# First batch's softmax and rows transposed on TensorE, its product in column blocks, its statistics as x lands

## The chip, the cores and the metric

The kernel runs on one core of a Trainium2 chip. The metric is the device time of one execution in microseconds, the median of three runs. The profile is one further execution, taken by the hardware profiler. Its times are microseconds from the start of the span. The engines are called PE (TensorE), DVE (VectorE), ACT (ScalarE), POOL (GpSimd) and SP (SyncE, which here only issues DMAs).

## The reference

The model is one block: a cross-attention whose keys come from a context, then an attention and mixture-of-experts block. There are four batches of 512 rows and 512 features. Cut to what matters:

```python
def xattn(logits, features, Wq, bq, Wk, bk):        # logits (4,512,512), features (4,512,256)
    query = features @ Wq.T + bq                    # 128 features
    key = features @ Wk.T + bk
    attention = softmax(query @ key.T, axis=-1)     # (512, 512)
    return einsum('bln,bmn->blm', logits, attention)

def ffn(hidden, ...):
    h = rmsnorm(hidden, ln1_w)
    q, k, v = h @ wq, h @ wk, h @ wv                # 16 heads of 128
    ao = causal_softmax(q @ k.T / sqrt(128)) @ v @ wo
    x = hidden + ao
    t = rmsnorm(x, ln2_w)
    # 16 experts, the best 6 of each row, and a shared expert
    return x + routed(t) + shared(t)

x = x + xattn(layernorm(x), ctx)
x = x + ffn(layernorm(x), ...)
```

## The kernel before, in words

Each number is held as a pair of 16-bit halves, a high half and a remainder. `split` makes the pair: ACT writes the high half, DVE the remainder. A product of two pairs takes three matmuls (`mm3`). Biases and scales ride along.

**Cross-attention, `xattn(b)`.** This is a Python generator, one for each batch; `step(b, n)` runs it for n yields. Its work for a batch is, in order: split the context (`ctp`); project queries and keys (tiles `xq`, `xqk`); bring in x turned, in two halves (`turned`), and make its pair `lnp` (`turn`: the high half on ACT, the remainder on POOL); four energies (`en`), each with a maximum on DVE, an exponential on ACT, a reciprocal and a split into `pn`; `pn` turned into `ptp`, here by a DMA transpose that SP issues (`flip`). `stats` takes mean and variance of the rows of x with DVE (`bn_stats`, four tiles), lets POOL take the power -1/2, and makes `nb`. `center` adds `nb` to x on POOL. Then four products `xm` of `lnp` with `ptp`, each followed by an update of x, a second layer norm (`mv`, `r`, `hu`, `hd`), and the normalised rows as a pair `hh`, which is turned into `hT` by `flip`. Products share the two PSUM banks with the tag w; banks a and s have three each.

**Heads.** The attention loop runs over 64 heads of four batches, first those of batches 0 and 1. `queries`, `values`, `scores`, `attend` and `project` are its stages. `fetch` brings in the weights of a head the first time: a load into a staging tile, `split`, and a write of the pair to a scratch tensor in HBM (`wqk_d`, `wv_d`, `wo_d`), from which later batches read. The staging pool `stg` has two tiles with the tag st. The context of a batch, both halves of its turned x (batch 0's turned x apart) and the weights take turns in them, so a load waits until the last reader of the tile before is through.

**What sets the order.** The kernel is written as one program, and a scheduler puts the instructions into one fixed queue for each engine. `after(ins, first)` adds an order between two instructions. SP's queue carries loads and transposes, POOL's queue carries POOL's own arithmetic and the scratch writes. `warm` issues matmuls with no use of their result. Batch 0 runs through the generator at once (`step(0, 99)`), then the small loads (`ln2b`, `zrow`, `g32`, `gtp`) and the first nine yields of batch 1 are issued, and batch 1's last twelve yields follow two for each of the first six heads. The loop of head 0 splits `values` and `queries` in halves, so that the first half needs only half of `hT`.

Of the kernel before, what the change touches and what calls it, by code (L numbers as in the profile page):

```python
# [9 lines left out]
F16 = mybir.dt.float16  # L10
F32 = mybir.dt.float32
# [44 lines left out]
def xattn_moe_block_kernel(ctx: ExitStack, tc: tile.TileContext, x, xT, ctxT, wqkx, bqk, ln1, ln2,  # L56
# [32 lines left out]

    def flip(o, i):  # L90
        return nc.sync.dma_start_transpose(out=o, in_=i)

    def after(ins, first):
        tc.add_manual_dep(ins.ins, first.ins.name,
# [90 lines left out]
    def warm(n, first=None):  # L185
        ps = bank("w", "warm")
        for _ in range(n):
            ins = nc.tensor.matmul(ps, onesm, zero, start=True, stop=True)
            if first:
                after(ins, first)  # L190

    warm(10)
    ct0 = ctx_load(0)
    wx32 = at_.tile([P, 2 * CC * P], F32, tag="f", name="wx32")
# [8 lines left out]
    def xattn(b):  # L203
# [4 lines left out]
            nc.sync.dma_start(t, xT[b, j])  # L208
            return t

        if b == 0:
            xT32 = [turned(j) for j in range(2)]
        xt = (ap_ if b else x2p).tile([P, NT, D], F32, tag="xt" if b else "x2", name=f"xt{b}")
        nc.sync.dma_start(xt, x[b].rearrange("(t p) d -> p t d", p=P))
        if b == 0:
            nc.sync.dma_start(ln1b, ln1.partition_broadcast(P))
            for nm, src in (("wqk0", wqk[0]), ("wv0", wv[0])):
                t = vp.tile([P, NT, 2, GW], F16, tag="vt", name=f"{nm}_st")
                early_st[nm] = t.rearrange("p t a d -> p (t a d)").bitcast(F32)
                nc.sync.dma_start(early_st[nm], src)  # L220
        ctp = ap_.tile([P, 2, CC, S], F16, tag="lnp", name="ctp")
        for j, ins in enumerate(split(ctp[:, 0], ctp[:, 1], ct32, HS)):
            if b == 1:
                after(ins, zz["calm"][j])
        spare = dict(pm=[(he, "pe3"), (xp, "h2"), (he, "pe3"), (xp, "x1t")],
                     pn=[(hq, "qk0"), (hq, "qk1"), (he, "pn3"), (rp, "h2p")], hh=[(he, "pn3"), (rp, "h2p")])
        spare.update(hu=spare["pm"], qf=spare["pm"])
# [21 lines left out]
        def stats():  # L249
            mv = asm.tile([P, NT, 2], F32, name="mvs", bufs=2)  # L250
            for m in range(NT):
                st = asm.tile([P, 6], F32, name="st")
                ins = nc.vector.bn_stats(st, xt[:, m, :])
                if b < 2:
                    after(ins, zz["hh", 0] if b else zz["sm", 0][1])
                nc.vector.bn_aggr(mv[:, m, :], st)
            ins = nc.vector.tensor_scalar(rs, mv[:, :, 1], 1e-5, PS * PS, ALU.add, ALU.mult)
            if b == 0:
                zz["calm"] = zz["sm", 0][0], ins
            nc.gpsimd.tensor_tensor(rs, rs, mhalf, ALU.pow)  # L260
            ins = nc.vector.scalar_tensor_tensor(nb, mv[:, :, 0], -PS, rs, ALU.mult, ALU.mult)
            if b == 0:
                zz["nb"] = ins

        def center(t):
            nc.gpsimd.tensor_scalar(xt[:, t, :], xt[:, t, :], nb[:, t:t + 1], None, ALU.add)
# [21 lines left out]
        if b == 0:  # L288
            warm(8, zz["xq"])
            for j in range(2):  # L290
                turn(j, xT32[j])
        else:
            lnp = wide("lnp")
        yield
        for m in range(NT):
            ml = slice(m * P, (m + 1) * P)
            if b:
                if m < 2:
                    turn(m, turned(m))
                elif m == 2:  # L300
                    stats()
                else:
                    for t in range(NT):
                        center(t)
                yield
            ps = bank("s", f"en{b}_{m}")
            last = mm3(ps, [(qk[0][:, 0, ml], qk[0][:, 1, ml], qk[1][:, 0], qk[1][:, 1])])
            nm = asm.tile([P, 1], F32, name="nm")
            ins = nc.vector.tensor_reduce(nm, ps, AX.X, ALU.max, negate=True)
            if b == 1:  # L310
                after(ins, zz["hh", 0])
            pm = tmp("pm", F32)
            sm = asm.tile([P, 1], F32, name="sm")
            nc.scalar.activation(pm, ps, AF.Exp, bias=nm, accum_out=sm)
            rc = asm.tile([P, 1], F32, name="rc")
            nc.vector.reciprocal(rc, sm)
            nc.vector.tensor_scalar(rc, rc, PS, None, ALU.mult)
            pn, hi, lo = pair(tmp("pn", F16))
            zz["sm", b] = split(hi, lo, pm, rc)
            zz["ptp", b] = flip(ptp[:, :, ml], pn)  # L320
            yield
        if b == 0:
            stats()
            after(nc.vector.tensor_scalar(ln1b, ln1b, HS, None, ALU.mult), zz["calm"][1])
            for t in range(NT):
                center(t)
            warm(22, last)
        if b < 2:
            x2s[b] = x2p.tile([P, NT, D], F32, tag="x2", name="x2")
        hT[b] = hpool.tile([P, 2 * C, S], F16, tag="hT", name=f"hT{b}")  # L330
        for t in range(NT):
            ps = bank("w", f"xm{b}_{t}")
            tl = slice(t * P, (t + 1) * P)
            xv = xt[:, t, :]
            zz["xm", b, t] = mm3(ps, [(lnp[:, c, tl], lnp[:, C + c, tl], ptp[:, c], ptp[:, C + c]) for c in range(C)])
            nc.vector.scalar_tensor_tensor(xv, ps, rs[:, t:t + 1], xv, ALU.mult, ALU.add)
            q = nc.gpsimd if b else nc.sync
            q.dma_start(x1_d[b][:, t, :], xv)
            st = asm.tile([P, 6], F32, name="st")
            nc.vector.bn_stats(st, xv)  # L340
            mv = asm.tile([P, 2], F32, name="mv")
            nc.vector.bn_aggr(mv, st)
            r2 = asm.tile([P, 2], F32, name="r2")
            nc.vector.tensor_scalar(r2[:, 0:1], mv[:, 1:2], 1e-5, None, ALU.add)
            nc.vector.tensor_scalar(r2[:, 1:2], mv[:, 1:2], 1.0 + 1e-6, 1e-11, ALU.mult, ALU.add)
            nc.gpsimd.tensor_tensor(r2, r2, mhalf[:, :2], ALU.pow)
            hu = tmp("hu", F32)
            nc.vector.scalar_tensor_tensor(hu, xv, mv[:, 0:1], ln1b, ALU.subtract, ALU.mult)
            yield
            nb = asm.tile([P, 1], F32, name="nb")  # L350
            nc.vector.scalar_tensor_tensor(nb, mv[:, 0:1], -1.0, r2[:, 0:1], ALU.mult, ALU.mult)
            hd = x2s[b][:, t] if b < 2 else tmp("hd", F32)
            nc.gpsimd.tensor_scalar(hd, xv, r2[:, 0:1], nb, ALU.mult, ALU.add)
            if b >= 2:
                q.dma_start(hid_d[b][:, t, :], hd)
            if stop == "A":
                nc.sync.dma_start(out[b, tl], hd)
            yield
            hh, hi, lo = pair(tmp("hh", F16))
            zz["hh", b] = split(hi, lo, hu, r2[:, 1:2])[1]  # L360
            zz["hT", b] = flip(hT[b][:, :, tl], hh)
            yield

    if stop == "A":
# [7 lines left out]
        for _ in range(n):  # L372
            next(bg[b], None)

    step(0, 99)
    ln2b = const.tile([P, D], F32, name="ln2b")
    nc.sync.dma_start(ln2b, ln2.partition_broadcast(P))
    after(nc.vector.tensor_scalar(ln2b, ln2b, HS, None, ALU.mult), zz["calm"][1])
    zrow = xp.tile([1, D], F32, tag="x1t", name="zrow", bufs=1)
    nc.vector.memset(zrow, 0.0)  # L380
    nc.gpsimd.dma_start(y_d[0:1, :], zrow)
    nc.gpsimd.dma_start(yo_d[0:1, :], zrow)
    g32 = const.tile([P, C * E], F32, name="g32")
    nc.sync.dma_start(g32, gate)
    gtp = const.tile([P, 2, C, E], F16, name="gtp")
    gtf = gtp.rearrange("p a c e -> p a (c e)")
    for j, ins in enumerate(split(gtf[:, 0], gtf[:, 1], g32, WS)):
        after(ins, zz["calm"][j])
    step(1, 1 + 2 * NT)

    shx = {}

# [13 lines left out]
    def fetch(b, g, pool, tag, n, src, scr, nm):  # L406
# [10 lines left out]
        if first:  # L417
            st_ = early_st[nm]
        else:
            st_ = stg.tile([P, 1024], F32, tag="st", name=f"{nm}_st")  # L420
            ins = nc.sync.dma_start(st_[:, :n], src)
            if nm == "wqk1":
                after(ins, zz["hT", 0])
        for j, ins in enumerate(split(w[:, 0], w[:, 1], st_[:, :n], WS)):
            if first:
                after(ins, zz["nb"] if j else zz["calm"][0])
        ins = (nc.sync if nm == "wqk0" else nc.gpsimd).dma_start(scr, w.rearrange("p a n -> p (a n)"))
        if nm != "wqk0":
            zz["pad"] = ins
        if nm == "wqk0":  # L430
            after(ins, zz["ptp", 0])
        return w

    pieces = []
# [300 lines left out]
    for n in range(NH + LAG + 1):  # L735
        if n < NH:
            b, h = heads[n]
            if b not in opened:
                opened.add(b)
                step(b, 99)  # L740
                if b == B - 1:
                    shared_pool()
            parts = [queries(b, h)]
            if h % HG == 0:
                parts.append(values(b, h // HG))
            if n == 0:
                parts.reverse()
                for p in parts:
                    next(p)
            for p in parts:  # L750
                for _ in p:
                    pass
# [28 lines left out]
        if H // 2 <= n < H // 2 + E:  # L781
            pad_rows(n - H // 2)
        if n < 6:
            step(1, 2)
        else:
            for _, j in zip(range(2 - n % 2), bring):
                step(j)
# [441 lines left out]
```

## Time and profile before

| what | value |
|---|---|
| median of three runs | 1832.03 us (1832.01 to 1837.33) |
| profiled execution | 1838.93 us |
| its span, first to last instruction | 1837.2 us |
| mean granted clock of TensorE | 0.974 |
| TensorE busy | 1739.6 us, 95% |
| VectorE busy | 1113.9 us, 61% |
| ScalarE busy | 829.5 us, 45% |
| GpSimd busy | 444.8 us, 24% |

The page cuts the span into 40 slices of 46 us and gives each engine's busy share of a slice in tenths. A row of the timeline has the start, the length, the engine, the line of the kernel, the operation, what it writes and reads, and in brackets the idle time of the engine before it with what ended it. A row of the waits has the waiting instruction, what it waited for, the total, the number and the longest. Where a helper such as `split` or `mm3` records the instruction, the line is that of the helper, and the tile tells whose it is.

### The profile page before, as it was taken

The page shows a single profiled execution, that of the slowest core. Times are in us where ns is not written, and L with a number is a line of the kernel's source. Part 1 is how long each engine was busy: PE and PEld are TensorE (multiplying, and loading weights), DVE is VectorE, ACT ScalarE, POOL GpSimd, SP SyncE. Part 2 cuts the span into 40 slices and gives each one's busy share as a digit, 9 for nine tenths or more (in the row PEclk, how much of TensorE's full clock was granted, in tenths as well). Part 3 has the DMA queues.
Part 4 walks back from the last instruction along what each step waited for, and adds up shares of the span by engine and source line. Part 5 has one row for each costly group of instructions (what it writes and reads, how often), then busy time and mean ns, then how long its engine had stood idle before and what let it go on. Part 6 is the DMA issues. An engine that isn't in the chain of part 4 may idle for free. (4 is left out here: it accounts for less than half of the span.)

```text
span 1837.2 us, 27581 instructions
## 1 busy us (share of the span) xinstructions
PE 1739.6 (95%) x9919; PEld 937.2 (51%) x9919; DVE 1113.9 (61%) x2766; ACT 829.5 (45%) x1711; POOL 444.8 (24%) x522
## 2 busy tenths in 40 slices
PE   7899999999986998999999979899999999999998
PEld 3455555555543554645655534345555555555453
DVE  6887777777673774756667625554444434446755
ACT  4555645465432543535445423234444444544431
POOL 5423011130345235000003334400000000025564
PEclk9899999999997998999999989899999999999999
DMA  7977768674675677654437534566454655579766
GB/s 235 228 165 215 160 144 191 159 185 93 136 161 159 151 168 212 134 101 91 86 68 150 130 107 102 199 178 177 138 155 144 178 147 147 148 223 252 217 206 209
DMA packets 392723, 296.23 MB, mean 161 GB/s; under 512 B 334880, under 2 KB 335136, under 8 KB 391808
## 3 DMA queue, kind: packets, MB, share of 16 engines
q1 hardware_dynamic: 359456, 180.32, 42.0%
q0 software_dynamic: 33120, 114.06, 19.6%
q8 instruction: 80, 1.31, 0.3%
q14 instruction: 67, 0.55, 0.1%
HBM read 124.81 MB, written 88.94 MB: 116 GB/s over the span
## 5 line engine op out<-in xcount | busy, mean ns | idle before, releaser
L1105 POOL DMA_INDIRECT yg<-y_d,yrc x96 | 110.5, 1151 | 535.8 <-DVE hf L1008 455.6
L630 ACT ACTIVATE pe<-pe,bnm 128x128 f32<-128x128 f32 (+3 forms) x256 | 142.4, 557 | 161.1 <-DVE bnm L628 156.4
L83 PE MATMUL qk<-hT,wqk 128*128 128x512 f16 (+1 forms) x520 | 197.8, 380 | 5.0 <-DMA hT<-hh 3.8
L86 PE MATMUL qk<-hT,wqk 128*128 128x512 f16 (+1 forms) x520 | 197.9, 381 | 1.1 <-issue 1.1
L87 PE MATMUL qk<-hT,wqk 128*128 128x512 f16 (+1 forms) x520 | 197.8, 380 | 1.1 <-issue 1.1
L74 DVE SCALAR_TENSOR_TENSOR pn<-pe,brc,pn 128x128 f16<-128x128 f32 (+3 forms) x256 | 146.7, 582 | 21.9 <-ACT pn L73 18.6
L628 DVE CUSTOM_DVE_ANT_0 pe<-sc,causal 128x128 f32<-128x128 f32 (+3 forms) x256 | 117.4, 486 | 64.0 <-PE sc L625 57.2
L86 PE MATMUL v<-wv,hT 128*128 128x256 f16 x512 | 141.6, 276 | 6.5 <-issue 6.5
L83 PE MATMUL v<-wv,hT 128*128 128x256 f16 x512 | 141.5, 276 | 6.4 <-issue 5.5
L73 ACT ACTIVATE pn<-pe,brc 128x128 f16<-128x128 f32 (+3 forms) x256 | 133.5, 553 | 30.1 <-ACT pe L630 16.3
L87 PE MATMUL v<-wv,hT 128*128 128x256 f16 x512 | 141.5, 276 | 4.9 <-issue 4.7
L83 PE MATMUL g<-xT,wt 128*128 128x384 f16 (+2 forms) x384 | 127.3, 331 | 0.0
L86 PE MATMUL g<-xT,wt 128*128 128x384 f16 (+2 forms) x384 | 127.3, 331 | 0.0
L87 PE MATMUL g<-xT,wt 128*128 128x384 f16 (+2 forms) x384 | 127.2, 331 | 0.0
L994 ACT ACTIVATE hT_e<-hf 128x384 f16<-128x384 f32 (+3 forms) x96 | 51.1, 532 | 143.9 <-DVE hf L1008 136.2
L73 ACT ACTIVATE qkt<-qk 128x512 f16<-128x512 f32 x128 | 75.0, 588 | 90.5 <-PE qk L87 85.0
L83 PE MATMUL y<-dt,hT_e 128*128 128x512 f16 (+1 forms) x288 | 109.4, 380 | 0.0
L87 PE MATMUL y<-dt,hT_e 128*128 128x512 f16 (+1 forms) x288 | 108.9, 378 | 0.0
L86 PE MATMUL y<-dt,hT_e 128*128 128x512 f16 (+1 forms) x288 | 108.9, 378 | 0.0
L662 DVE SCALAR_TENSOR_TENSOR x<-wo,x 128x512 f32<-128x512 f32 x128 | 87.5, 687 | 32.5 <-PE wo L87 31.4
L74 DVE SCALAR_TENSOR_TENSOR qkt<-qk,qkt 128x512 f16<-128x512 f32 x128 | 87.7, 686 | 28.6 <-ACT qkt L73 24.0
L455 POOL DMA_INDIRECT xs_d<-h2p,slotu x96 | 95.3, 993 | 28.2 <-issue 28.2
(320 smaller groups left out, 4019.8 us busy)
## 6 DMA issues: line engine op xcount, KB each, us to landing
y_d<-yt SPq DMA_DIRECT2D x96, 256.0 KB
est<-in_ew_dram SPq DMA_DIRECT2D x32, 704.0 KB
est<-in_ed_dram SPq DMA_DIRECT2D x16, 768.0 KB
wqk<-wqk_d POOLq DMA_DIRECT2D x20, 512.0 KB
wqk_st<-in_wqk_dram SPq DMA_DIRECT2D x16, 512.0 KB
wqk_d<-wqk POOLq DMA_DIRECT2D x15, 512.0 KB
xs_d<-causal POOLq DMA_DIRECT2D x16, 384.0 KB
wv<-wv_d POOLq DMA_DIRECT2D x10, 512.0 KB
```

Of the source, the lines that this page charges most:

```text
L73: return (nc.scalar.activation(hi, src, AF.Copy, scale=scale), nc.vector.scalar_tensor_tensor(lo, src, scale, hi, ALU.mult, ALU.subtract))
L74: nc.vector.scalar_tensor_tensor(lo, src, scale, hi, ALU.mult, ALU.subtract))
L83: ins = nc.tensor.matmul(o, lh, rh, start=start and j == 0, stop=False)
L86: nc.tensor.matmul(o, lh, rl, start=False, stop=False)
L87: ins = nc.tensor.matmul(o, ll, rh, start=False, stop=stop and j == n - 1)
L455: ins = nc.gpsimd.indirect_dma_start(out=xs_d, out_offset=bass.IndirectOffsetOnAxis(ap=slotu[:, tt, k:k + 1], axis=0), in_=h2ps[tt], in_of ...
L628: nc.vector.tensor_tensor_reduce(pe, ps[:, :w], causal[:, S - w:], -1.0, 3e38, ALU.add, ALU.min, nm)
L630: nc.scalar.activation(pe, pe, AF.Exp, bias=nm, scale=-1.0, accum_out=sm)
L662: nc.vector.scalar_tensor_tensor(x2[:, t, :], ps, 1.0 / (VS * WS), x2[:, t, :], ALU.mult, ALU.add)
L994: nc.scalar.activation(hT[:R, ic, :w], hf, AF.Copy)
L1105: nc.gpsimd.indirect_dma_start(out=yg, out_offset=None, in_=src, in_offset=bass.IndirectOffsetOnAxis(ap=idx[:, tt, k:k + 1], axis=0))
```

## The change

Eight transposes of batch 0 leave the DMA: `pn` and `hh` are transposed by matmuls with an identity (`swap`), a high and a low half of four 128-column pieces each into a bank, and copied from PSUM by ACT and DVE (`pn`) or by ACT alone (`hh`). The first two products of batch 0 are issued in blocks of 128 columns as `ptp` comes in, the other two in whole rows from banks s. x of batch 0 is loaded ahead of its turned form, and `stats` of batch 0 is called before the energies. The second run of warm matmuls has 12 instead of 22. The head loop now starts after eleven yields of batch 0; the rest of it, the small loads and the first nine yields of batch 1 are put into `second_half()`, which is called after the first halves of head 0's `values` and `queries`. The yields of batch 1 by head change from 2,2,2,2,2,2 to 0,3,3,2,2,2. Several `after` orders are changed to match.

```diff
+    def swap(o, i, tag, low):
+        done = []
+        for a, put in enumerate((nc.scalar.copy, low)):
+            ps = bank(tag, "swap")
+            for c in range(C):
+                j = (a * C + c) * P
+                nc.tensor.matmul(ps[:, c * P:(c + 1) * P], i[:, j:j + P], id16, start=True, stop=True)
+            done.append(put(o[:, a * C:(a + 1) * C, :], ps.rearrange("p (c q) -> p c q", c=C)))
+        return done
...
+    id16 = ap_.tile([P, P], F16, name="id16")
+    nc.vector.tensor_copy(id16, ident)
...
-        if b == 0:
-            xT32 = [turned(j) for j in range(2)]
         xt = (ap_ if b else x2p).tile([P, NT, D], F32, tag="xt" if b else "x2", name=f"xt{b}")
         nc.sync.dma_start(xt, x[b].rearrange("(t p) d -> p t d", p=P))
         if b == 0:
+            xT32 = [turned(j) for j in range(2)]
...
             if b == 1:
-                after(ins, zz["calm"][j])
+                after(ins, zz["hh", 0] if j else zz["hi", 0])
...
-                if b < 2:
-                    after(ins, zz["hh", 0] if b else zz["sm", 0][1])
+                if b == 1:
+                    after(ins, zz["hh", 0])
...
             for j in range(2):
                 turn(j, xT32[j])
+            stats()
...
-            zz["ptp", b] = flip(ptp[:, :, ml], pn)
+            if b:
+                flip(ptp[:, :, ml], pn)
+            else:
+                zz["calm"] = swap(ptp[:, :, ml], pn, "a", nc.vector.tensor_copy)
             yield
         if b == 0:
-            stats()
             after(nc.vector.tensor_scalar(ln1b, ln1b, HS, None, ALU.mult), zz["calm"][1])
+            after(zz["nb"], zz["sm", 0][1])
             for t in range(NT):
                 center(t)
-            warm(22, last)
+            warm(12, last)
...
+        early_xm = [bank("w", f"xm{b}_{t}") for t in range(0 if b else 2)]
+        for m in range(NT):
+            ml = slice(m * P, (m + 1) * P)
+            for t, ps in enumerate(early_xm):
+                tl = slice(t * P, (t + 1) * P)
+                zz["xm", b, t] = mm3(ps[:, ml], [(lnp[:, c, tl], lnp[:, C + c, tl], ptp[:, c, ml], ptp[:, C + c, ml])
+                                                 for c in range(C)])
+        if b == 0:
+            early_xm += [product(t, "s") for t in range(2, NT)]
...
-            zz["hT", b] = flip(hT[b][:, :, tl], hh)
+            if b:
+                flip(hT[b][:, :, tl], hh)
+            else:
+                swap(hT[b][:, :, tl], hh, "as"[t // 2], nc.scalar.copy)
...
-    step(0, 99)
+    step(0, 5 + 6)
...
+    def second_half():
+        step(0, 99)
+        nc.sync.dma_start(ln2b, ln2.partition_broadcast(P))
...
+        step(1, 1 + 2 * NT)
...
-            ins = nc.sync.dma_start(st_[:, :n], src)
-            if nm == "wqk1":
-                after(ins, zz["hT", 0])
+            nc.sync.dma_start(st_[:, :n], src)
         for j, ins in enumerate(split(w[:, 0], w[:, 1], st_[:, :n], WS)):
             if first:
-                after(ins, zz["nb"] if j else zz["calm"][0])
+                after(ins, zz["calm"][j])
...
-                step(b, 99)
+                if n:
+                    step(b, 99)
...
                 for p in parts:
                     next(p)
+                second_half()
...
         if n < 6:
-            step(1, 2)
+            step(1, (0, 3, 3, 2, 2, 2)[n])
```

More of the change, by code (lines that the diff above doesn't have):

```diff
@@ L253, in stats @@
                 ins = nc.vector.bn_stats(st, xt[:, m, :])
-                if b < 2:
-                    after(ins, zz["hh", 0] if b else zz["sm", 0][1])
+                if b == 1:
+                    after(ins, zz["hh", 0])
                 nc.vector.bn_aggr(mv[:, m, :], st)
             ins = nc.vector.tensor_scalar(rs, mv[:, :, 1], 1e-5, PS * PS, ALU.add, ALU.mult)
-            if b == 0:
-                zz["calm"] = zz["sm", 0][0], ins
             nc.gpsimd.tensor_tensor(rs, rs, mhalf, ALU.pow)
-            ins = nc.vector.scalar_tensor_tensor(nb, mv[:, :, 0], -PS, rs, ALU.mult, ALU.mult)
-            if b == 0:
-                zz["nb"] = ins
+            zz["nb"] = nc.vector.scalar_tensor_tensor(nb, mv[:, :, 0], -PS, rs, ALU.mult, ALU.mult)
         def center(t):
@@ L330, in xattn, with product @@
         hT[b] = hpool.tile([P, 2 * C, S], F16, tag="hT", name=f"hT{b}")
+        def product(t, tag):
+            ps = bank(tag, f"xm{b}_{t}")
+            tl = slice(t * P, (t + 1) * P)
+            zz["xm", b, t] = mm3(ps, [(lnp[:, c, tl], lnp[:, C + c, tl], ptp[:, c], ptp[:, C + c]) for c in range(C)])
+            return ps
+        early_xm = [bank("w", f"xm{b}_{t}") for t in range(0 if b else 2)]
+        for m in range(NT):
+            ml = slice(m * P, (m + 1) * P)
+            for t, ps in enumerate(early_xm):
+                tl = slice(t * P, (t + 1) * P)
+                zz["xm", b, t] = mm3(ps[:, ml], [(lnp[:, c, tl], lnp[:, C + c, tl], ptp[:, c, ml], ptp[:, C + c, ml])
+                                                 for c in range(C)])
+        if b == 0:
+            early_xm += [product(t, "s") for t in range(2, NT)]
         for t in range(NT):
-            ps = bank("w", f"xm{b}_{t}")
             tl = slice(t * P, (t + 1) * P)
             xv = xt[:, t, :]
-            zz["xm", b, t] = mm3(ps, [(lnp[:, c, tl], lnp[:, C + c, tl], ptp[:, c], ptp[:, C + c]) for c in range(C)])
+            ps = product(t, "w") if b else early_xm[t]
             nc.vector.scalar_tensor_tensor(xv, ps, rs[:, t:t + 1], xv, ALU.mult, ALU.add)
@@ L359, in xattn @@
             hh, hi, lo = pair(tmp("hh", F16))
-            zz["hh", b] = split(hi, lo, hu, r2[:, 1:2])[1]
-            zz["hT", b] = flip(hT[b][:, :, tl], hh)
+            zz["hi", b], zz["hh", b] = split(hi, lo, hu, r2[:, 1:2])
+            if b:
+                flip(hT[b][:, :, tl], hh)
+            else:
+                swap(hT[b][:, :, tl], hh, "as"[t // 2], nc.scalar.copy)
             yield
@@ L373, in step @@
             next(bg[b], None)
-    step(0, 99)
+    step(0, 5 + 6)
     ln2b = const.tile([P, D], F32, name="ln2b")
[L377 to L382, printed above, removed]
     g32 = const.tile([P, C * E], F32, name="g32")
-    nc.sync.dma_start(g32, gate)
     gtp = const.tile([P, 2, C, E], F16, name="gtp")
     gtf = gtp.rearrange("p a c e -> p a (c e)")
-    for j, ins in enumerate(split(gtf[:, 0], gtf[:, 1], g32, WS)):
-        after(ins, zz["calm"][j])
-    step(1, 1 + 2 * NT)
+    def second_half():
+        step(0, 99)
+        nc.sync.dma_start(ln2b, ln2.partition_broadcast(P))
+        after(nc.vector.tensor_scalar(ln2b, ln2b, HS, None, ALU.mult), zz["hh", 0])
+        zrow = xp.tile([1, D], F32, tag="x1t", name="zrow", bufs=1)
+        nc.vector.memset(zrow, 0.0)
+        nc.gpsimd.dma_start(y_d[0:1, :], zrow)
+        nc.gpsimd.dma_start(yo_d[0:1, :], zrow)
+        nc.sync.dma_start(g32, gate)
+        for j, ins in enumerate(split(gtf[:, 0], gtf[:, 1], g32, WS)):
+            after(ins, zz["hh", 0] if j else zz["hi", 0])
+        step(1, 1 + 2 * NT)
     shx = {}
@@ L429, in fetch @@
             zz["pad"] = ins
-        if nm == "wqk0":
-            after(ins, zz["ptp", 0])
         return w
```

## The prediction

> **What bounds the kernel now.** I read the page first, then TensorE's waits in the first 110 us, then the timeline of the other engines there. The page says that TensorE is the bound:
>
> ```profile
> span 1837.2 us, 27581 instructions
> ...
> PE 1739.6 (95%) x9919; PEld 937.2 (51%) x9919; DVE 1113.9 (61%) x2766; ACT 829.5 (45%) x1711; POOL 444.8 (24%) x522
> ...
> PE   7899999999986998999999979899999999999998
> ...
> PEclk9899999999997998999999989899999999999999
> ```
>
> TensorE is busy 95%, nearly all of it with full slices. So a saving or a loss counts as time in which TensorE stands without work, or runs at half clock, or does added work. All that the change touches lies before 230 us; after that the kernels do the same work in TensorE's order, so a shift at 230 us stays until the end. The waits of TensorE up to 110 us (total, times, longest):
>
> ```profile
> PE xm L83 <- DMA ptp<-pn: 6.0, 1, 6.0
> PE xm L83 <- issue: 5.2, 1, 5.2
> PE qk L83 <- DMA hT<-hh: 3.5, 1, 3.5
> ...
> PE v L83 <- DMA hT<-hh: 0.9, 1, 0.9
> ```
>
> Three are transposes by DMA of batch 0 (ptp, hT), which the change aims at; the 5.2 is batch 1's product at 82.8 us, which nothing here moves to TensorE. Behind each longer one the clock halves: 128x512 matmuls follow each other at 0.427 us instead of 0.216 (8 of them from 25.96), 128x256 at 0.213 instead of 0.109 (15 from 52.8), again 10 from 82.84: 1.7 + 1.6 + 2.1 us lost. What stands ready beside it, from the timelines of GpSimd, SP and ScalarE:
>
> ```profile
> 44.70 2.12 POOL L273 TENSOR_TENSOR lnp<-xT,lnp 128x1024 f16<-128x1024 f32 x1
> ...
> 48.62 2.12 POOL L273 TENSOR_TENSOR lnp<-xT,lnp 128x1024 f16<-128x1024 f32 x1
> ...
> 59.64 7.45 POOL L266 TENSOR_SCALAR xt<-xt,nb 128x512 f32<-128x512 f32 x4 [0.50 <-DVE nb L261]
> ```
>
> ```profile
> 47.53 2.62 SPq L91 DMA_TRANSPOSE hT<-hh  x2
> 50.24 1.02 SPq L421 DMA_DIRECT2D wqk_st<-in_wqk_dram  x2
> ```
>
> ```profile
> 67.16 1.06 ACT L73 ACTIVATE wqk<-wqk_st 128x1024 f16<-128x1024 f32 x1 [1.18 <-DMA wqk_st<-in_wqk_dram]
> ...
> 78.13 1.06 ACT L73 ACTIVATE wqk<-wqk_st 128x1024 f16<-128x1024 f32 x1 [3.10 <-DMA wqk_st<-in_wqk_dram]
> ```
>
> Batch 1's turned x (lnp) leaves the two staging buffers before its centring, so the weights of heads 1 and 2 are fetched at 50.24. A fetch takes 3.7 us to use when the queue is free (issued 63.45, used 67.16) and 8.3 when it is full (69.79 to 78.13).
>
> **What the Trainium skill says.** "TensorE: Matmul & The Clock Gate", "What's actually happening": the clock halves after an idle window of about 3.4 us; the trace agrees (0.427 us against 0.216). "Perfetto Trace Analysis", "Tensor Engine Instruction": ScalarE, VectorE and GpSimd are strict FIFO; the trace agrees, e.g. ScalarE's 3.10 us wait above with scores behind it. "DMA: Bandwidth & Descriptors", "Queues, rings and completion order": an SDMA engine takes descriptors in ring order; agreeing, an early 512 KB load is used 3.7 us after issue and one behind writes 8.3. "SBUF — State Buffer", "Who interferes with whom": VectorE and GpSimd lock each other out of a shared port; the trace shows centring at 1.55 to 2.05 us for one shape, so GpSimd's times are soft.
>
> **The change part by part.** The order in which the built kernel's instructions stand per engine gives the queues; durations are the rows'.
>
> *A. Batch 0 up to its hidden rows.* Added: 64 matmuls of 128 columns (32 for ptp, 32 for hT). Three 128x128 score matmuls of the trace start 0.055 apart, so 3.5 us. The copies, 128x512 from PSUM, are not in the trace; nearest are 0.58 (ScalarE, vt) and 0.67 (VectorE, vt), bounds 0.4 to 0.8: 12 on ScalarE, 4 on VectorE. Products in 128-column blocks: same columns, 0. Removed: 8 DMA transposes (1.3 us each on SP), 10 warm matmuls. The statistics now stand on VectorE ahead of the query/key remainders, waiting for x. x moves ahead of xT: it is the third large load, so it lands when the second half of xT does today, about 9.0 us (1.83 MB have moved by 8.15 in the one-microsecond windows, and the first load was used 0.75 after its bytes). The statistics last 2.86 (19.29 to 22.15), so the remainders begin at 11.9 instead of 10.0, and the energies run 1.3 us later; behind the wait stand the maxima and the whole softmax. Bounds 0.8 to 2. GpSimd's power now precedes lnp's remainders (+1.2), hidden by the softmax.
> Then: the last high half ends at 19.7, ScalarE copies at 0.5 follow, VectorE's four copies stand among remainders and end near 24 to 25. The first two products end at 28, the other two at 33.3 (before 38.9). The last update of x starts at 34.8 instead of 39.15; the same chain of 8.9 us (39.15 to 48.1) and 0.4 + 4 x 0.5 for swap and copies instead of 3.9 for flip lead to about 45.4 for the second half of q/k, not 52.0. But 20 matmuls of batch 1 (11 xq, 9 en, 4.3 us) that lay in front of it are now behind it, and 1.6 of half clock after it goes: 52.0 - 4.3 + 1.6 - 45.4 = 3.9. **A = -4** (-8 to -2).
>
> *B. Batch 1's softmax moves in front of head 1.* second_half() issues all of it after head 0's first projection: statistics, the split of ctp, gate and ln2 loads, zero rows, energies, four maxima and exponentials, four normalisations, four flips. TensorE has 11.8 us of work from 45.4 (24 qk, 11 xq, 24 v, 12 en, 12 sc), but the energies wait for remainders and for three score banks that the exponentials free: about 4 us of gaps and 1 of half clock, so it runs dry at 62.3. Head 1's weights are late: on GpSimd the power of batch 1 comes at 48.5 (statistics 2.5, ctp 1.2, others 1.7 after 43), then four centrings at 2.05 until 58.1, a DMA issue 0.55, and only now lnp's first remainder, to 60.8, which frees the staging buffer. SP has two flips first, so the load starts at 62.0, lands 4 later; ScalarE, through with eight exponentials and eight high halves at 66.8, adds 1.05: 67.8. TensorE waits 5.5. Before, head 1 started at 59.6 without head 0's scores (1.6): 61.2 for equal work. 67.8 - 61.2 is 6.6, on top of the 4 already won: **B = +10.7** (+5 to +13).
>
> *C. Heads 1 to 3.* Loads, their scratch writes (512 KB each) and flips meet as today, but in a shorter stretch. wv1 is issued at 71.5 behind flips and a write, 6 to 8 us, and ScalarE waits for it ahead of head 1's keys. I put 3.0 for v, 0.7 + 2.3 + 1.1 + 0.4 for scores and flips, two half-clock windows of 1.7: 10.9. Gone: 5.2 + 2.1, as the product now stands where ptp has landed. **C = +3** (-5 to +6).
>
> *D. Batch 1's rows.* Its product steps follow 10 us later, and on ScalarE and VectorE wo2's split, on SP the 1 MB load of batch 2's x, now stand ahead of the last hh and flip. hT1 lands near 157; q/k of batch 1 started at 140.9 with a wait of 0.3, and would be ready near 152.5. Wait 4.5, half clock up to 3.4: **D = +7.6** (0 to +9).
>
> The ln2, gate and zero-row instructions are only moved and lie beside TensorE's work in B; if that cover goes they cost 1.3 us on VectorE, counted there.
>
> Sum: -4 + 10.7 + 3 + 7.6 = +17. The profiled execution took 1838.9 (its span 1837.2 and 1.7 around it), so 1856; the median of the three runs is 6.9 lower, 1832.0, so **1849 us**.
>
> **Rivals.** *Faster: transfers land quickly.* Eight flips are off the SP queue; if every load lands within 3 us, head 1's weights come before 62.3 (B +5), the product's 5.2 + 2.1 go with nothing in their place (C -7) and D is 0: -6, 1826; with more of the gaps filled 1822. It decides at 62.3: weights there by then. For it: the DMA rows of 40 to 50 us are light. Against: the staging buffer frees only at 60.8, whatever the queue.
> *Break-even:* B at its low end, C and D nothing: +1, 1833. For it: GpSimd centres at 1.55, not 2.05, when VectorE is off its port.
> *Worse:* GpSimd and VectorE lock more in B, and hT1 is later: +26, 1858 and above.
> *Not what it says* is out: the swaps, blocks and moved steps stand in the built order.
>
> **How the numbers follow.** Forecast 0.62, worse 0.14, break-even 0.10, faster 0.14. 0.3% (5.5 us) is about what a measurement of this kernel can tell from no change: slower 0.76, same 0.10, faster 0.14. The unknown ends reach from -8 to +30; leaving out the outer tenths gives 1830 to 1862.
>
> **What would show it.** Right: x used near 9 us; the first product near 22; second half of q/k near 45; POOL's lnp remainders of batch 1 after its centring, the load of head 1's weights after 60, TensorE waiting near 62 to 68; a wait for hT near 150. Wrong: head 1 follows head 0's scores without a gap, or the clock stays full through 55 to 70.

## The result: slower, about as the profile was forecast, above the range of the median

The changed kernel took 1864.72 us (median of four, 1857.19 to 1868.51), the kernel before 1833.71 (median of four, 1832.01 to 1837.33). The ratio is 1.0161, interval 1.0125 to 1.0198. A ratio is worked out from the executions and not from the two medians, and it leaves out those that took over 1.5% longer than the fastest of their kernel. The prediction was 1849, range 1830 to 1862: right side and right places, but the median lies above the range. The profiled execution took 1857.19 us, where 1856 was worked out.

The page of the changed kernel, its span, TensorE's busy time, and busy share and clock by slices:

```profile
span 1855.5 us, 27828 instructions
...
PE 1748.9 (94%) x10045; PEld 942.6 (51%) x10045; DVE 1117.0 (60%) x2771; ACT 835.5 (45%) x1723; POOL 438.6 (24%) x522
...
PE   8799999999986998989999989899999999999998
...
PEclk9899999999997998999999989899999999999999
```

The slices hardly differ from those of before. What changed shows in TensorE's waits up to 250 us (the waiting instruction, what it waited for, total, times, longest):

```profile
PE qk L83 <- ACT wqk L73: 5.6, 1, 5.6
PE sc L650 <- ACT pm L322: 4.8, 2, 3.4
PE qk L83 <- DMA hT<-hh: 3.9, 1, 3.9
...
PE en L86 <- DVE xqk L293: 2.3, 1, 2.3
```

The waits for ptp (6.0), for batch 1's product (5.2) and for batch 0's hT (3.5) are gone. In their place stand head 1's weights (5.6, until 69.3 us), head 0's scores shortly before (3.4, released by an exponential of batch 1, `pm`) and batch 1's hT (3.9, until 156.0):

```profile
69.26 0.61 PE L83 MATMUL qk<-hT,wqk 128*128 128x512 f16 x1 [5.61 <-ACT wqk L73]
...
155.95 0.38 PE L83 MATMUL qk<-hT,wqk 128*128 128x512 f16 x1 [3.85 <-DMA hT<-hh]
```

The trace's clock shows half speed from 57.5 to 74.6, 98.4 to 101.9 and 156.5 to 159.9.

To see where time goes for good, I compare the start of the same matmul in both profiles ("position" below). The changed kernel stands 9.5 us later at 130 us, 15.1 at 155, 10.4 at 230, 11.9 at 255, still 11.4 at 1650, and its span ends 18.3 later.

Now the queues at 49 to 69 us, GpSimd first (start, length, engine, line, operation, what it writes and reads):

```profile
49.10 6.19 POOL L273 TENSOR_SCALAR xt<-xt,nb 128x512 f32<-128x512 f32 x4 [0.30 <-DVE nb L270]
55.24 0.64 POOL L516 DMA_DIRECT2D x1t<-x_d  x1
55.91 4.21 POOL L280 TENSOR_TENSOR lnp<-xT,lnp 128x1024 f16<-128x1024 f32 x2
```

VectorE and SP in the same profile:

```profile
57.08 3.60 DVE L74 SCALAR_TENSOR_TENSOR pn<-pm,rc,pn 128x512 f16<-128x512 f32 x1
```

```profile
60.70 2.73 SPq L91 DMA_TRANSPOSE ptp<-pn  x2
63.53 0.53 SPq L452 DMA_DIRECT2D wqk_st<-in_wqk_dram  x1
```

The centrings now stand ahead of lnp's remainders, as forecast. But the first remainder ends at 58.0 and so frees the staging buffer there, not at 60.8: four centrings took 6.19, not 4 x 2.05. The load still starts at 63.53. Ahead of it on SP stand two flips, and they wait until 60.70 for pn, whose remainder took VectorE 3.60 us where the same operation takes 0.75 to 1.18 when GpSimd makes no remainder. It ends at 60.68, 0.56 after GpSimd's second remainder.

### The profile page after: what moved, and what is told of

It reads as the page before. It is cut to its first block, busy times and chain, and to the rows that moved or that the text cites. A ratio compares the mean times of both kernels' runs of the same rounds, so it can differ in the third digit from the quotient of the medians.

```text
span 1855.5 us, 27828 instructions
## 1 busy us (share of the span) xinstructions
PE 1748.9 (94%) x10045; PEld 942.6 (51%) x10045; DVE 1117.0 (60%) x2771; ACT 835.5 (45%) x1723; POOL 438.6 (24%) x522
```

## The experiments

Ratios are to the kernel before on the same chip, with 95% intervals. The chips differ (the kernel before takes 1796 to 1800 us on three, 1834 to 1839 in the first runs and on a further chip), so only times of one chip are subtracted. Executions of one kernel on one chip lie some 15 to 40 us apart, so the position from one profile and the median of many are given side by side. Where nothing else is said, a position is against the first profile of the kernel before, also for runs on other chips: what the chips differ in lies behind 500 us (last section).

**again: nothing edited.**

> The changed kernel, unaltered, for a second profile and more times. Theory (the first 230 us cost +10 to +12, and what a run takes beyond that comes from the last 200 us, where gathered rows are added up): median 1860 to 1868; TensorE's work at 230 us stands 10 to 12 us later than in the kernel before, as in the first profile, and what this execution has more than 1857.2 arises after 230 us. Rival (the waits at 58 to 69 us and at 156 us differ from run to run with the clock's windows): the shift at 230 us differs from 10 to 12 by 3 us or more, and it accounts for the excess.

Measured: 1812.71 against 1795.95, ratio 1.0118 (1.0074 to 1.0163). The same waits (5.6, 3.5, 3.7). Position +6.1 at 230, +9.0 at 265 us. The chip is faster, so the first expectation's absolute numbers don't apply; the waits repeat, while the position differs by 3 to 4 us from that of the first profile. About half of this is the stretch of half clock at 98 us, which this profile lacks. That is nearer the rival for the shift, but the front alone does not explain 17 us, and the theory's loss in the last 200 us isn't there either (position -31.3 at 1650 us, -32.2 at the end; the large minus is the chip's).

**half_back: the softmax of batch 1 where it was.**

```diff
-    step(0, 5 + 6)
+    step(0, 99)
...
+    second_half()                     # and without its own step(0, 99)
...
-                second_half()
...
-            step(1, (0, 3, 3, 2, 2, 2)[n])
+            step(1, 2)
```

> The changed kernel with batch 1's softmax, the gate and ln2 loads and the zero rows issued where the kernel before issues them (all of batch 0, then this, then head 0; two steps of batch 1 per head). Swaps, column blocks and the statistics as x lands stay. Theory (B and D of the prediction, the moved softmax, are the loss; A is a gain of 4): 1825 to 1834, the wait for head 1's weights near 65 us and the one for hT near 156 us gone. Rival (the swaps, their copies and the early statistics are the loss): over 1850, little below the changed kernel. Second rival (the tail after 1650 us is the loss and has nothing to do with the front): 1840 to 1850.

Measured: 1806.73, ratio 1.0074 (1.0045 to 1.0102). GpSimd's and VectorE's timelines:

```profile
50.97 6.20 POOL L273 TENSOR_SCALAR xt<-xt,nb 128x512 f32<-128x512 f32 x4 [1.68 <-DVE nb L270]
57.11 0.64 POOL L517 DMA_DIRECT2D x1t<-x_d  x1
57.78 4.21 POOL L280 TENSOR_TENSOR lnp<-xT,lnp 128x1024 f16<-128x1024 f32 x2
```

```profile
59.87 3.35 DVE L74 SCALAR_TENSOR_TENSOR pn<-pm,rc,pn 128x512 f16<-128x512 f32 x2 [0.26 <-ACT pn L73]
```

TensorE's wait for head 1's weights falls from 5.6 to 2.1, and that for hT near 156 is gone; the position is +5.5 at 265 us, where again's is +9.0. So the moved softmax carries a part of the loss. But the kernel does not come back to the level of the one before, and as a whole none of the three expectations holds: the ratio alone is one that the second rival allows (1840 to 1850 against 1834), yet its cause, a loss after 1650 us, is not in the profile. The moved softmax is not what turns GpSimd's order round: with it back in place, centring still comes first, pn is still slow (3.35 for two, the first some 2.7), and the load of head 1's weights still starts late, at 65.4. Batch 0's rows are done some 6 us sooner than before, so batch 1's statistics are ready sooner too (nb at 48.8 in the changed kernel, 59.4 before), while ScalarE's high halves of lnp come 9 us later (50.6 against 41.5). That the scheduler turned the order for this reason is argued, not tried.

**lnp_first: GpSimd's order of batch 1 put back, nothing else.**

```diff
-            nc.gpsimd.tensor_tensor(lo, t, hi, ALU.subtract)
+            zz["low", b] = nc.gpsimd.tensor_tensor(lo, t, hi, ALU.subtract)
...
+            if b == 1:
+                after(ins, zz["low", 1])          # ins: a centring
```

> The changed kernel, with GpSimd's two remainders of batch 1's turned x (lnp) put ahead of its four centrings, so that the staging buffers come free some 6 us sooner. Theory (head 1's weights are late because the staging buffer frees late; 5.6 us of wait and 2 to 3 of half clock hang on it): 7 to 9 below the changed kernel, 1855 to 1858 where that stands at 1865; the wait for wqk near 69 us is gone or under 1 us. Rival (the queue's two flips in front of the load, which wait for the normalised rows, hold it): the wait shrinks by less than 2 us and the time by less than 3.

Measured: 1793.37, ratio 0.9990 (0.9967 to 1.0013), 19.3 below the changed kernel on its chip: more than twice what the theory asked. GpSimd, then SP:

```profile
52.82 4.20 POOL L282 TENSOR_TENSOR lnp<-xT,lnp 128x1024 f16<-128x1024 f32 x2 [1.28 <-ACT lnp L279]
57.02 7.73 POOL L273 TENSOR_SCALAR xt<-xt,nb 128x512 f32<-128x512 f32 x4
```

```profile
54.97 2.41 SPq L454 DMA_DIRECT2D wqk_st<-in_wqk_dram  x2
58.90 1.37 SPq L91 DMA_TRANSPOSE ptp<-pn  x1
```

TensorE's wait for the weights in the list of waits:

```profile
PE qk L83 <- ACT wqk L73: 0.6, 1, 0.6
```

The weights are asked for at 55.0 and pn takes 0.74. The wait of 5.6, that of 3.4, the long half clock and batch 1's wait for hT are all gone. The position against the kernel before is -8 to -9 near 95 us and -6.3 at 265. So one order on an engine that is 24% busy decides whether the change costs some 1% or nothing that can be measured.

**rows_early: batch 1's rows asked for a head sooner.**

```diff
-            step(1, (0, 3, 3, 2, 2, 2)[n])
+            step(1, (0, 3, 3, 3, 3, 0)[n])
```

> The changed kernel with batch 1's twelve row steps spread over heads 1 to 4 (three each) and not over heads 1 to 5, so that its last hidden rows and their flip come a head sooner. Theory (D: 3.9 us of wait for hT near 156 us and half clock behind it): 4 to 6 below the changed kernel. Rival (the steps take ScalarE's and VectorE's time from the scores of heads 3 and 4, and the wait only moves): within 2 of it.

Measured: ratio 1.0072 (1.0038 to 1.0106), the wait for hT still 3.6. SP's queue shows why this tells nothing about D:

```profile
146.02 0.38 SPq L224 DMA_DIRECT2D xt<-in_x_dram  x1
...
149.22 1.89 SPq L91 DMA_TRANSPOSE hT<-hh  x1
```

The last flip stands where it stood (149.12 in the changed kernel): the scheduler kept its order. The median is lower than again's by 2, with overlapping intervals.

**wg: batch 1's turned x in two idle buffers, so that staging is free.**

```diff
-            t = (stg if b else wg).tile(..., tag="st" if b else "wo", name="xT32")
+            t = (stg if b > 1 else wg).tile(..., tag="st" if b > 1 else "wo", name="xT32")
```

> The changed kernel with batch 1's turned x fetched into the two idle buffers of the output weights (as batch 0's is), so that head 1's weights find a free staging buffer at once; GpSimd still centres before it makes lnp's remainders. Theory (the late weights of head 1 are the main loss): no wait for wqk near 69 us, 8 to 12 below the changed kernel, ratio to the kernel before 1.004 to 1.010. Rival (the main loss is VectorE, held off by GpSimd's remainders: two pn halves took 2.1 us each there and not 0.75): the wait of the scores near 61 us (3.4) and the slow pn stay, wherever the remainders run, and the ratio stays at 1.010 or above.

Measured: 1812.39 against 1798.69, ratio 1.0066 (1.0040 to 1.0092). No wait for wqk is left, pn takes 0.74 (the remainders run elsewhere in this build), and the position at 120 us is -2 (single matmuls between 100 and 140 lie further off, as the order differs in part). Then, from the list of waits:

```profile
PE qk L83 <- DMA hT<-hh: 8.4, 1, 8.4
```

With the heads ahead and the rows not, batch 1's hT is waited for twice as long, 10.2 us of half clock around it, and the position at 170 is +10. Taking one wait away only moved it: D is a limit of its own. The ratio lies where the theory put it, but not by its path alone; the changed kernel was not run on this chip, so the 8 to 12 us are not tested.

**x2_late: batch 2's x behind the last flip.**

```diff
+        if b == 2:
+            after(ins, zz["flip", 1])             # ins: the load of x
```

> The changed kernel with batch 2's load of x (1 MB) put behind batch 1's last flip of hidden rows on SP; before, it stood in front. Theory (the transfer in front makes the flip land 6.7 us after its issue where it took 3.0 before): the wait for hT near 156 us falls from 3.9 to under 1.5, and the time by 3 to 6 against the changed kernel. Rival (the flip is slow because other weights load beside it): the wait stays above 3.

Measured: 1804.27, ratio 1.0025 (0.9998 to 1.0052). SP, then the wait:

```profile
147.30 2.00 SPq L91 DMA_TRANSPOSE hT<-hh  x1
149.53 1.15 SPq L224 DMA_DIRECT2D xt<-in_x_dram  x1
```

```profile
PE qk L83 <- DMA hT<-hh: 2.4, 1, 2.4
```

The wait falls from 3.9 to 2.4, between the two expectations, and the flip is used 5.4 us after its issue, where it took 6.8 in the changed kernel and 6.7 in again: the load in front is part of it. That other weights are the rest is not shown. The ratio lies further below the changed kernel's on the other chips (1.0064 to 1.0161) than the wait can give (the position at 265 is +7.3, again's +9.0); that excess is not explained.

**lnp_fliphh and lnp_stats: two parts of A undone, on top of lnp_first.**

```diff
-                swap(hT[b][:, :, tl], hh, "as"[t // 2], nc.scalar.copy)
+                flip(hT[b][:, :, tl], hh)          # lnp_fliphh, batch 0 too
```

> The kernel lnp_first with batch 0's hidden rows transposed by DMA again, 4 flips for 32 swaps and 8 copies; all else stays. Theory (A: swap and copies take 2.4 us after the last hidden rows where a flip takes 3.9 and stands in a queue): the second half of head 0's projection starts 3 to 6 later than in lnp_first, ratio to the kernel before 1.001 to 1.004. Rival (head 1's weights come no sooner, so what is won there is lost at head 1): within 2 us of lnp_first.

```diff
                 turn(j, xT32[j])
-            stats()
...
+            stats()                                # lnp_stats: behind the softmax and in its old order
```

> The kernel lnp_first with batch 0's layer norm statistics where the kernel before has them, behind the softmax. Theory (A: as x lands they hold the energies by some 2 us, and this is not won back): the wait for xqk near 14 us is gone, the swaps start 1 to 2 earlier, and the time falls by 1 to 2. Rival (behind the softmax the statistics hold up the copies, the centring and the first update of x instead): 2 to 4 above lnp_first.

Measured: lnp_fliphh 1798.62, ratio 0.9996 (0.9975 to 1.0017); lnp_stats 1796.77, ratio 0.9986 (0.9959 to 1.0013). The new wait of each, in that order:

```profile
PE v L83 <- DMA hT<-hh: 5.0, 1, 5.0
```

```profile
PE swap L99 <- ACT hh L73: 4.7, 2, 4.4
```

With flips the first half of the values waits 5.0, but the second half of q/k starts at 45.9 against 45.1 in lnp_first: at 265 us the position is 1.3 later than lnp_first's, the rival's size. With the statistics behind the softmax the wait for xqk is gone, and the swaps of hh wait instead: 4.6 later than lnp_first's. Both medians are level with lnp_first, so each part of A is worth 1 to 5 us in a profile and nothing that the medians resolve.

**before_a, after_b, before_b, after_c: both kernels twice on one chip.**

> The kernel before, unaltered, profiled beside the changed one on one chip. Theory (the loss lies in the first 260 us; behind it both kernels run alike and only the clock's windows differ by chance): against the changed kernel's profile of the same chip TensorE's work stands 8 to 13 us earlier at 260 us, and the idle time of TensorE from 260 us to the end differs by less than 4. Rival (the changed kernel loses again later, at the flips of the probabilities and the gathered rows): its idle time after 260 us is 6 or more above that of the kernel before in both pairs.

> The changed kernel, unaltered, beside before_a. Theory (front only): 9 to 15 above the kernel before, ratio 1.005 to 1.008. Rival (later as well): ratio 1.012 or more, with 6 or more of idle time and half clock after 260 us in this profile and in after_c.

> The kernel before once more, to see how far two executions of one kernel differ after 260 us: both theories expect idle times there within 4 of before_a; if they differ by 6 or more, single profiles cannot tell the theories apart after 260 us, and only the medians can.

> The changed kernel once more. Theory (front only): TensorE's position at 260 us is 8 to 13 later than in the kernel before, as in after_b; idle time after 260 us within 4 of the kernel before. Rival: as in after_b.

| kernel | median (lowest to highest) | ratio | profile: idle TensorE after 260 us |
|---|---|---|---|
| before_a | 1840.45 (1823.24 to 1848.94) | 0.9994 (0.9968 to 1.0021) | 70.5 |
| before_b | 1838.38 (1830.40 to 1855.70) | 1.0012 (0.9987 to 1.0036) | 63.5 |
| after_b | 1861.35 (1846.36 to 1869.55) | 1.0098 (1.0063 to 1.0132) | 65.4 |
| after_c | 1853.24 (1840.75 to 1870.02) | 1.0064 (1.0041 to 1.0087) | 70.8 |

The positions at 265 us are +13.8 and +14.1 (after_b), +17.6 and +17.9 (after_c) against the two profiles of before. That is more than the 8 to 13 that the theory put. The idle time after 260 us cannot tell the kernels apart: it differs by 7.0 between the two profiles of the kernel before, more than the 6 from which on single profiles were to be held unable to decide (in the two first profiles it was 64.6 and 69.9). What is left are the positions and the medians. From 265 to 1650 us the position changes by -7.9 to +6.3 in the four pairs, by -0.8 in the mean, so no later loss is seen, though one of a few microseconds would not be. The medians lie 14 and 22 us above that of the kernel before, 18 in the mean, and the positions at 265 are 16 in the mean. So nearly all of the loss is made in the first 260 us; the ratios, 1.0064 and 1.0098, lie below the rival's 1.012, one of them above the theory's 1.008.

**before_center: only GpSimd's order, in the kernel before.**

```diff
+            if b == 1:
+                for j in range(2):
+                    after(zz["low", 1, j], ins)   # ins: a centring
```

> The kernel before, with nothing of the change but GpSimd's order of batch 1 turned round: the four centrings ahead of lnp's two remainders. Theory (this order alone carries the loss, through the staging buffers and head 1's weights): the weights, fetched at 50 us before, are fetched after 66; TensorE waits 8 to 15 us for them near 65 to 80, and the ratio to the kernel before is 1.006 to 1.012. Rival (the order matters only together with the swaps and the moved softmax): within 0.3% of the kernel before.

Measured: 1811.92 against 1799.66, ratio 1.0070 (1.0046 to 1.0094), position +9.4 at 265 us. GpSimd, then SP, then ScalarE at the weights:

```profile
58.11 6.66 POOL L266 TENSOR_SCALAR xt<-xt,nb 128x512 f32<-128x512 f32 x4 [2.11 <-DVE rc L319]
64.74 4.59 POOL L276 TENSOR_TENSOR lnp<-xT,lnp 128x1024 f16<-128x1024 f32 x2
```

```profile
64.77 6.37 SPq L91 DMA_TRANSPOSE pt<-pn  x4
71.23 1.01 SPq L424 DMA_DIRECT2D wqk_st<-in_wqk_dram  x2
```

```profile
75.20 1.06 ACT L73 ACTIVATE wqk<-wqk_st 128x1024 f16<-128x1024 f32 x1 [9.64 <-DMA wqk_st<-in_wqk_dram]
```

The weights are asked for 21 us later (71.2 against 50.2) and ScalarE waits 9.6 us for them. VectorE is held off here too, at the probabilities whose flips stand ahead of the load (the same three operations take 1.67 in the changed kernel):

```profile
64.47 5.41 DVE L74 SCALAR_TENSOR_TENSOR pn<-pe,brc,pn 128x256 f16<-128x256 f32 x3 [0.21 <-ACT pn L73]
```

In this build TensorE's queue has batch 1's product ahead of head 1, so its waits read "xm <- ptp" (5.9) and "av <- pt" (2.9) and not "wqk": the 8 to 15 us for the weights that the theory put are not there as such. The one edit, with what the scheduler made of it, costs 12 us, with no swap and no moved softmax; by which of these waits is not separated.

**ctp_early: the loads ahead of the flips.**

```diff
-                after(ins, zz["hh", 0] if j else zz["hi", 0])
+                after(ins, zz["calm"][j])
```

> The changed kernel with batch 1's context split where ScalarE and VectorE have just copied batch 0's last turned probabilities, not behind its last hidden rows. In the built order the centrings still stand first, but the loads for heads 1 and 2 now stand ahead of the two flips. Theory (the staging buffer decides, the flips add to it): head 1's weights land 2 to 4 us sooner, the wait near 69 us falls from 5.6 to 2 to 4, ratio 1.005 to 1.008. Rival (the flips, which wait for VectorE, decide): the wait is gone, ratio 1.004 or less.

Measured: 1801.39, ratio 0.9998 (0.9972 to 1.0024). GpSimd, then SP:

```profile
50.93 6.18 POOL L273 TENSOR_SCALAR xt<-xt,nb 128x512 f32<-128x512 f32 x4
57.09 4.20 POOL L280 TENSOR_TENSOR lnp<-xT,lnp 128x1024 f16<-128x1024 f32 x2
```

```profile
59.23 2.42 SPq L452 DMA_DIRECT2D wqk_st<-in_wqk_dram  x2
62.01 3.53 SPq L91 DMA_TRANSPOSE ptp<-pn  x2
```

Centring still stands first, yet the load leaves at 59.2, when the first remainder frees its buffer, and the wait for wqk is gone: the rival's outcome. pn starts as the remainders end and takes 0.75. So with the same order on GpSimd the load is on time once it stands ahead of the pair of flips: in the changed kernel it was the flips that held it last, and behind these VectorE. This single profile stands at +7.4 at 265 us (a flip of head 1's probabilities was waited for 5.5 us at 103), while 22 executions are level with the kernel before.

**lnp_first_b: lnp_first on another chip.**

> The kernel lnp_first once more, beside the others. Theory (with GpSimd's order restored the change gains 3 to 8 us in the first 260 us and keeps them): ratio 0.996 to 0.999. Rival (the gain is given back later): 0.999 to 1.002. Both expect TensorE 3 to 9 us ahead of the kernel before at 260 us.

Measured: 1792.30 against 1799.66, ratio 0.9983 (0.9958 to 1.0008); position -4.1 at 265. Together with lnp_first, weighted by the intervals, 0.9987 (0.9970 to 1.0004): level, or a few microseconds ahead. It beats the changed kernel; that it beats the kernel before is likely and not shown.

## Why the prediction was right or wrong

**A, -4: right.** x was used at 9.96 (forecast near 9), the first product came at 21.5 (22), the last update of x at 34.4 (34.8), the second half of q/k at 44.0 (45.4). By the prediction's own working, A is -5.3. The statistics put the first maximum off by 2.2 (14.8 against 12.5), where 1.3 was put; the rest more than made up for it. The rows of the changed kernel, VectorE's and then TensorE's:

```profile
9.96 2.47 DVE L264 BATCH_NORM_STATS2 st<-xt 128x6 f32<-128x512 f32 x4 [2.46 <-DMA xt<-in_x_dram]
...
34.42 0.74 DVE L361 SCALAR_TENSOR_TENSOR xt<-xm,rs,xt 128x512 f32<-128x512 f32 x1
```

```profile
44.01 0.38 PE L83 MATMUL qk<-hT,wqk 128*128 128x256 f16 x2 [0.59 <-ACT hT L100]
```

**B, +10.7: right place and nearly the size, with the wrong last link.** TensorE ran dry at 63.7 (62.3), head 1 started at 69.3 (67.8); 69.3 - 61.2 is 8.1, and with A taken off B is +13.4, just above its range of 5 to 13. lnp_first shows that the loss goes with the order of GpSimd, before_center that this order brings a loss of 12 us without the rest of the change, and ctp_early that the order does so only while the flips stand ahead of the load. The failed link is "which frees the staging buffer": that came at 58.0. What held the load were the two flips ahead of it, and these waited for VectorE, locked out by GpSimd's remainder. That the size came out was luck: two errors nearly cancelled, centrings of 1.55 priced at 2.05 and a pn of 3.60 priced at 0.75. The 2.05 was the mean of four centrings of batch 0, of which one took 3.53 and three 1.55. I had named the lock, but put it into the worse rival as a vague "lock more"; the trace of before already held its price, a `nb` of 0.15 that took 2.08 at 44.76 beside a remainder of 2.12. "SBUF — State Buffer", "Who interferes with whom", in the Trainium skill says which pairs to look for: "A DVE instruction with two SBUF inputs contends with a GpSimd instruction that reads SBUF". The profiles agree: pn (two SBUF inputs) is slow, while the maxima, read from PSUM, keep 0.63 beside the same remainders in lnp_first.

**C, +3: right in sign and small.** The position is +9.5 at 130 us, so C is +1.4. (The prediction's own terms give 10.6 for B and 3.6 for C, so its sum should read +17.8.)

**D, +7.6: right, somewhat high.** The wait for hT came at 152.1 to 156.0, 3.9 (forecast 4.5), and the position rose by 5.6 with its half clock. wg shows D as a limit of its own; x2_late shows the 1 MB load as part of it.

**"A shift at 230 us stays until the end": right on the whole.** The sum at 155 us was +15.1 for a forecast of +17. It fell by 4.7, to 10.4, at 230. About half of this is a stretch of half clock of the kernel before (at 189) that its two later profiles lack; against these it falls by 2.1 to 2.4. Over four profiles of the changed kernel and three of before the mean position at 265 is +13.5, and nothing systematic follows up to 1650 us. That the profiled execution met 1856 so closely is luck: 6.9 of its 18.3 us arose after 1650 us, where the prediction had nothing, and in the pairs with before_a the same stretch gave -3.1 and -5.9.

**The median: the term that failed.** The step that failed is the last one: the sum was made against one profiled execution and carried to the median by taking 6.9 off, from three runs 5 us apart. The other three executions of the changed kernel lay 7 to 11 us above its profiled one, not below; their granted clock was 0.968 to 0.971 against 0.974, which is 6 to 11 us more of lost clock. And the range let the causes vary but gave the executions no spread. They have one: 1840.75 to 1870.02 for the changed kernel and 1821.69 to 1851.99 for the kernel before on one chip, sixteen and 56 executions. Four against four gave +31. Over the four comparisons of the two unaltered kernels the mean, weighted by the intervals, is 1.0096, some 18 us of 1834, against +17 forecast; the intervals of 1.0161 and 1.0064 do not overlap, so this mean is less sure than its parts (the three later ones give 1.0081, some 15 us), and what made the first comparison so large is open. Part of it all is the clock: span times one less the granted clock, averaged over the executions of the second chip, is 26.2 us for the kernel before, 31.1 for the changed one and 21.4 for lnp_first.

## What to carry over

When a wait is removed, list for each engine which instructions now become ready in another order, and follow the new order through buffers and queues to the next load; here two groups that changed places on the least busy engine cost more than the swaps on TensorE won. Before pricing a VectorE operation with two SBUF inputs, see what GpSimd runs beside it. Give a forecast of a median the spread of the executions, not only that of its causes.

## What was not expected of the hardware

A VectorE remainder of 0.75 us took 3.60 beside two GpSimd remainders of 2.12: it waited through the rest of one and all of the next, and did not get in between. That is no rule: in before_center two such operations, of 0.61 and 0.74 us elsewhere, took 2.37 and 2.61, and the first ended within GpSimd's second remainder. Beside centrings in lnp_first it took 0.74, 1.18 and 0.74, and the four centrings 1.56 to 2.63 each, where they take 1.55 to 1.57 in the changed kernel.

The same kernel differs by some 40 us between chips, in two stretches where TensorE waits for nothing that is shown. The waits of the kernel before at 500 to 640 us, in its first profile:

```profile
PE v L86 <- issue: 5.5, 8, 1.9
...
PE v L87 <- issue: 4.4, 6, 1.8
PE v L83 <- issue: 4.3, 6, 1.2
```

Such rows stand near 570 and 1070 us in all six profiles from the slower chips, with 27 to 31 us of half clock between 500 and 640 (7 to 17 on the faster ones), and in no profile from the faster chips. Both kernels have them alike.
